# One fetch of the fixed blocks' weights for two phases, and a routing softmax built on tanh

## The chip, the cores and the metric

The kernel runs on one core of a Trainium2 chip. The metric is the device time of one execution in microseconds (us). Below, PE is the TensorE matrix engine (PEld is its weight load), DVE is VectorE, ACT is ScalarE, POOL is GpSimd, and SP is SyncE, whose queue issues most DMA transfers. Line numbers such as L882 are lines of the kernel before.

## The reference

The kernel computes one decoder layer on 32 sequences of 128 tokens with width 128: causal self-attention with 16 heads of 8, cross-attention to a second input, and a mixture of 8 experts of which each token takes 2, each followed by a residual sum and a layer norm. The part that the change touches:

```python
def _moe(x, rw, rb, w1, b1, w2, b2):
    xf = x.reshape(T, D)                                        # 4096 tokens x 128
    router_weights = jax.nn.softmax(xf @ rw + rb, axis=-1)      # over 8 experts
    topw, topi = jax.lax.top_k(router_weights, K)               # K = 2
    topw = jax.nn.softmax(topw, axis=-1)
    combine = zeros((T, E)).at[arange(T)[:, None], topi].add(topw)
    h = gelu(einsum('td,edf->etf', xf, w1) + b1[:, None, :], approximate=False)
    eo = einsum('etf,efd->etd', h, w2) + b2[:, None, :]         # hidden width 512
    return einsum('etd,te->td', eo, combine)

x = layernorm(x + attn(x, x, x, causal=True))
x = layernorm(x + attn(x, encoder_output, encoder_output, causal=False))
x = layernorm(x + moe(x))
```

Each token's two weights are a softmax of the two largest softmax values.

## The kernel before

**Attention.** The 32 sequences form 8 groups of 4. For each group the kernel runs self-attention (`s`) and later cross-attention (`c`). A sequence of one kind is a unit, and the program walks through the units in half-slots (`half_slot`): each gives TensorE half of a new unit's scores (`sc`, L457, whose maxima `m` VectorE takes at L465), half of an older unit's transposed scores (`st`, L450, whose exponentials ScalarE takes at L473 into the tile `pr`), and the values or outputs of a still older one. All other steps of a group (transposes into `kvT`, keys `k`, queries, projection, norm, hand-over `xT0`, routing) are generators. `chain` and `book` put their pieces into half-slots by a table of estimated engine costs, and the emission order is then kept as it is: every engine works through its own instructions in that order.

**Routing.** After cross-attention, `route` (L608 to L653) computes the logits `lg`, their softmax (Exp at L622, normalization at L625 to L627), the largest values `top` and their places `idx`, and the two weights from the difference of the two largest values with Tanh (L640). `place` (L668 to L755) counts tokens per expert and gives each of a token's two rows a slot; `biases` forms `comb`, transposes it on TensorE (`pw`, L597), and writes the residual sum with the weighted expert biases to `x2d`. `scatter` sends rows to their slots in `xs` with indirect DMAs from GpSimd (L762). The routing of the last two groups is emitted beside the expert blocks.

**Blocks.** The groups form two phases of four. The rows of a phase fill 39 blocks of 128 rows. The first 8 blocks of each phase belong to the experts 0 to 7 in order (the fixed blocks, `i < NS`). The expert of each of the other 31 is known only from the routing, and SP reads it from `ph.tab` before it issues the fetch. A block's weights are one row of `wpk` in HBM, packed early in the kernel: 1028 floats on each of 128 partitions, with the first layer, the second layer and 4 bias columns. `fetch_weights` (L822) brings them into a `wd` tile; that tag has `AHEAD + 1`, five, buffers. `Pipeline.run` fetches the weights of block `j + AHEAD`, issues the first layer of block `j` (`ph`, L866, and Gelu, L871), then the second layer of the block before (`po`, L882), which VectorE copies to `ot` (L887) and GpSimd sends to `eo` with an indirect DMA (L889). Rows are fetched (`xt`, L814) and transposed (`px`, L843, copied to `xT` at L858) four blocks at a time. `prepare` fetches the first four blocks' weights six half-slots before the blocks start. `combine` (L950) loads a group's results (`gt`), adds them with the two weights, applies the last norm and stores the output; it starts four blocks after the last block that its group needs.

Of the kernel before, what the change touches and what calls it, by code (L numbers as in the profile page):

```python
# [17 lines left out]
P = 128  # L18
# [35 lines left out]
def bc(ap, axis, n):  # L54

    ap = ap.unsqueeze(axis)
    shape = list(ap.shape)
    shape[axis] = n
    return ap.broadcast_to(shape)
# [3 lines left out]
def kernel(  # L63
# [544 lines left out]
    def route(gr):  # L608
# [11 lines left out]
        nc.vector.tensor_tensor(lg, lg, bc(lm, 2, E), ALU.subtract)  # L620
        yield
        nc.scalar.activation(lg, lg, AF.Exp)  # L622
        yield
        ls = small.tile([P, G], F32, tag="ls", name=f"ls_{gi}")
        nc.vector.tensor_reduce(ls, lg, AX.X, ALU.add)  # L625
        nc.vector.reciprocal(ls, ls)
        nc.vector.tensor_tensor(lg, lg, bc(ls, 2, E), ALU.mult)  # L627
        top = small.tile([P, G, E], F32, tag="top", name=f"top_{gi}")
        idx = small.tile([P, G, E], U32, tag="idx", name=f"idx_{gi}")
        for b in range(G):  # L630
            nc.vector.max(top[:, b, :], lg[:, b, :])
        yield
        for b in range(G):
            nc.vector.max_index(idx[:, b, :], top[:, b, :], lg[:, b, :])


        ex = small.tile([P, G], F32, tag="ex", name=f"ex_{gi}")
        nc.vector.tensor_tensor(ex, top[:, :, 0], top[:, :, 1], ALU.subtract)
        yield
        nc.scalar.activation(ex, ex, AF.Tanh, scale=0.5)  # L640
        idf = small.tile([P, G, 2], F32, tag="idf", name=f"idf_{gi}")
# [9 lines left out]
        yield  # L651
        nc.vector.tensor_scalar(wts[:, 0, bs], ex, 0.5, 0.5, ALU.mult, ALU.add)
        nc.vector.tensor_scalar(wts[:, 1, bs], ex, -0.5, 0.5, ALU.mult, ALU.add)  # L653

# [123 lines left out]
    def pack_biases():  # L778
        pb = mm_tile([P, E * NFC], "pb")
        nc.tensor.transpose(pb, b1, ident[: E * NFC, : E * NFC])  # L780
        b1T = setup.tile([P, E * NFC], F32, name="b1T")
        nc.vector.tensor_copy(b1T, pb)
        nc.sync.dma_start(
            out=wpk[:, :, B1:].rearrange("e p c -> p e c"),
            in_=b1T.rearrange("p (e c) -> p e c", c=NFC),
        )
# [8 lines left out]
    def weights(name):  # L795
        return moe.tile([P, 1, WP], F32, tag="wd", name=f"wd_{name}", bufs=AHEAD + 1)

    class Blocks:
# [23 lines left out]
        def fetch_weights(self, i):  # L822
            if i >= self.n:
                return
            wd = weights(f"{self.ph.p}_{i}")
            if i < NS:
                nc.sync.dma_start(out=wd[:, 0, :], in_=wpk[i])
            else:
                d = i - NS
                e = nc.sync.value_load(self.ph.tab[0:1, d : d + 1], min_val=0, max_val=E - 1)  # L830
                nc.sync.dma_start(
                    out=wd, in_=wpk[bass.ds(e, 1), :, :].rearrange("e p w -> p e w")
                )
            self.w[i] = wd[:, 0, :]

# [24 lines left out]
        def first_layer(self, i):  # L860
            w, name = self.w[i], f"{self.ph.p}_{i}"
            pool, tag = ((ps_sc, "sc"), (ps_st, "st"))[i % 2]
            hid = pool.tile([P, 2, NFC, P], F32, tag=tag, name=f"ph_{name}")[:, 0]
            self.h[i] = moe.tile([P, NFC, P], F32, tag="h", name=f"h_{name}")
            for c in range(NFC):
                nc.tensor.matmul(  # L866
                    hid[:, c, :], lhsT=w[:, c * P : (c + 1) * P],
                    rhs=self.xT[i // XB][:, i % XB, :], start=True, stop=True,
                )
            for c in range(NFC):  # L870
                nc.scalar.activation(  # L871
                    self.h[i][:, c, :], hid[:, c, :], AF.Gelu, bias=w[:, B1 + c : B1 + c + 1]
                )

        def second_layer(self, i):
            if i < 0:
                return
            q, p = i // XB, self.ph.p
            w, h = self.w.pop(i), self.h.pop(i)
            po = mm_tile([P, P], f"po_{p}_{i}")  # L880
            for c in range(NFC):
                nc.tensor.matmul(  # L882
                    po, lhsT=h[:, c, :], rhs=w[:, W2 + c * P : W2 + (c + 1) * P],
                    start=c == 0, stop=c == NFC - 1,
                )
# [14 lines left out]
    class Pipeline:  # L900


        def __init__(self, *blocks):
            self.all = [(k, i) for k in blocks for i in range(k.n)]
            self.quads = [(k, q) for k in blocks for q in range(-(-k.n // XB))]
            self.turned = 0

        def weights(self, j):
            if j < len(self.all):
                k, i = self.all[j]  # L910
                k.fetch_weights(i)

        def prepare(self):
            for j in range(AHEAD):
                self.weights(j)

# [13 lines left out]
        def run(self, beside):  # L930
# [3 lines left out]
            for j, (k, i) in enumerate(self.all):  # L934
                self.weights(j + AHEAD)
                k.first_layer(i)
# [192 lines left out]
    start = max(behind, ready)  # L1129
    at(start - 6, blocks.prepare)  # L1130
    at(start - 1, blocks.first_rows)

    def unit(t):
# [125 lines left out]
```

## Time and profile before

| | |
|---|---|
| runs, median (lowest to highest) | 683.09 us (679.27 to 684.35), 3 runs |
| the profiled execution | 683.11 us |
| its span, first to last instruction | 681.4 us |
| busy share of PE / DVE / ACT / POOL | 87% / 60% / 59% / 54% |
| chain that ended last | PE 59%, DVE 16%, ACT 9%, issue 6%, DMA 6% |
| blocks: first `ph` to the end of the last `po` | 458.93 to 660.83 us |
| phase two: its first `ph` | 578.83 us |
| weights of blocks | 78 transfers of 514 KB, 16 of them for fixed blocks |
| table loads of ScalarE beside blocks | five of 1.28 us, the first at 457.56 |

Lines of the timeline have the start in us, the length in us, the engine, the line and operation, the tiles (written <- read), shapes and a count of merged instructions; in square brackets stands how long the engine was idle before it and what ended that. "issue" means that nothing in the profile shows what it waited for. Lines by stretches of time have, for each engine, the busy us and the number of instructions, then the granted TensorE clock (1.00 is full), the mean busy share of the 16 DMA engines and the GB/s moved. The rows of 40 digits divide the span into slices of 17 us, in tenths of the clock granted and of the DMA engines' time.

### The profile page before, as it was taken

Reading aid. Unit: us, or ns where it says so; the run is one execution under the profiler, and the core shown is the slowest. Engines: PE = TensorE matmul, PEld = TensorE weight load, DVE = VectorE, ACT = ScalarE, POOL = GpSimd, SP = SyncE. Lnnn points to the kernel's source line nnn. Section 1 sums busy time; section 2 is a strip of 40 time slices with the busy share of each in tenths; the row PEclk is TensorE's granted clock in tenths of the full one; section 3 lists DMA queues with packets and bytes.
Section 4 is the critical chain, followed back from the end, with each engine's and each line's share of the span. In section 5 each row is a group of like instructions: output and inputs, shape, how many; then the busy total and the mean of one; then the engine's idle time right before and its main releaser. Section 6 shows DMA issues by size and latency. Waiting matters only on the chain.

```text
span 681.4 us, 21953 instructions
## 1 busy us (share of the span) xinstructions
PE 591.5 (87%) x8863; PEld 486.6 (71%) x8863; DVE 409.2 (60%) x1321; ACT 402.4 (59%) x919; POOL 368.0 (54%) x747
## 2 busy tenths in 40 slices
PE   8898898999998899989999888879888888999970
PEld 6666676777776666776776776768777688989870
DVE  2345555555668866795796786784664435553553
ACT  4166575686676567666767766554653355655651
POOL 3156554444545557447647435454766676555651
PEclk9699999899999999999999999998968899999995
DMA  6010701731010020001001000604667889999972
GB/s 139 20 34 3 137 20 37 201 135 58 2 34 2 11 64 11 2 22 37 26 2 57 10 3 18 218 14 152 209 213 219 299 274 366 371 371 356 356 262 76
DMA packets 48038, 82.48 MB, mean 121 GB/s; under 512 B 7968, under 2 KB 26464, under 8 KB 47936
## 3 DMA queue, kind: packets, MB, share of 16 engines
q1 hardware_dynamic: 42816, 71.57, 33.2%
q0 software_dynamic: 4544, 9.38, 3.8%
q8 instruction: 69, 1.13, 0.7%
q14 instruction: 33, 0.27, 0.1%
q10 hardware_dynamic: 576, 0.13, 0.1%
HBM read 62.15 MB, written 23.10 MB: 125 GB/s over the span
## 4 chain that ended last, share of the span: by engine, by line
PE 59%; DVE 16%; ACT 9%; issue 6%; DMA 6%; POOL 3%; SPq 1%; ACTq 0%; DVEq 0%; another core or an unknown queue 0%; POOLq 0%
PE ph L866 7%; PE po L882 7%; PE st_s L450 6%; PE st_c L450 5%; PE sc_s L437 4%; DVE m_s L465 4%; DMA wd<-wpk 4%; PE po_s L512 3%; DVE m_c L465 3%; PE po_c L512 3%; PE sc_c L457 3%; PE st_s L442 2%; ACT pr_s L473 2%; PE st_c L442 2%; PE sc_s L457 2%
## 5 line engine op out<-in xcount | busy, mean ns | idle before, releaser
L871 ACT ACTIVATE h<-ph,wd 128x128 f32<-128x128 f32 x312 | 88.0, 371 | 79.1 <-issue 45.6
L465 DVE TENSOR_REDUCE m_s<-sc_s 128x8 f32<-128x1024 f32 x64 | 78.3, 1224 | 84.8 <-PE st_s L450 65.0
L477 POOL TENSOR_SCALAR_AFFINE_SELECT pr_s<-pr_s 128x1024 f32<-128x1024 f32 x64 | 69.9, 1092 | 99.4 <-ACT pr_s L473 99.3
L889 POOL DMA_INDIRECT eo<-ot,to x78 | 78.5, 1007 | 66.2 <-DVE acc L974 15.0
L473 ACT ACTIVATE pr_s<-st_s 128x1024 f32<-128x1024 f32 x64 | 65.6, 1026 | 64.1 <-PE st_s L450 59.0
L473 ACT ACTIVATE pr_c<-st_c 128x1024 f32<-128x1024 f32 x64 | 65.7, 1027 | 59.1 <-PE st_c L450 53.7
L465 DVE TENSOR_REDUCE m_c<-sc_c 128x8 f32<-128x1024 f32 x64 | 78.0, 1219 | 32.6 <-PE st_c L450 19.6
L866 PE MATMUL ph<-xT,wd 128*128 128x128 f32 x624 | 89.5, 289 | 9.3 <-DMA wd<-wpk 3.8
L882 PE MATMUL po<-wd,h 128*128 128x128 f32 x624 | 88.1, 287 | 9.8 <-ACT h L871 7.4
L866 PEld LDWEIGHTS ph<-xT,wd 128*128 128x128 f32 x624 | 80.6, 202 | 15.2 <-issue 6.3
L882 PEld LDWEIGHTS po<-wd,h 128*128 128x128 f32 x624 | 80.7, 200 | 11.4 <-ACT h L871 8.6
L457 PE MATMUL sc_c<-k_c,qb_c 32*128 32x128 f32 x1024 | 75.3, 283 | 4.5 <-DVE m_c L465 4.1
L457 PE MATMUL sc_s<-k_s,qb_s 32*128 32x128 f32 x1024 | 78.1, 293 | 0.0
L887 DVE COPY ot<-po 128x128 f32<-128x128 f32 x78 | 22.6, 290 | 83.4 <-PE po L882 59.3
L762 POOL DMA_INDIRECT xs<-x,slots x64 | 64.3, 1005 | 12.7 <-issue 12.1
L450 PE MATMUL st_c<-qb_c,k_c 32*128 32x128 f32 x1024 | 70.2, 272 | 0.2 <-issue 0.2
L450 PEld LDWEIGHTS st_s<-qb_s,k_s 32*128 32x128 f32 x1024 | 69.7, 192 | 0.1
L450 PE MATMUL st_s<-qb_s,k_s 32*128 32x128 f32 x1024 | 69.6, 275 | 0.0
L450 PEld LDWEIGHTS st_c<-qb_c,k_c 32*128 32x128 f32 x1024 | 68.8, 187 | 0.9 <-issue 0.4
L457 PEld LDWEIGHTS sc_s<-k_s,qb_s 32*128 32x128 f32 x1024 | 65.5, 194 | 2.5 <-issue 2.1
L457 PEld LDWEIGHTS sc_c<-k_c,qb_c 32*128 32x128 f32 x1024 | 62.5, 185 | 6.1 <-DVE m_c L465 5.7
L437 PE MATMUL sc_s<-causal,ident 128*128 128x512 bf16 x128 | 39.7, 393 | 13.7 <-DVE m_s L465 10.3
(243 smaller groups left out, 1186.8 us busy)
## 6 DMA issues: line engine op xcount, KB each, us to landing
wd<-wpk SPq DMA_DIRECT2D x78, 514.0 KB
xs<-blank SPq DMA_DIRECT2D x2, 2600.0 KB
xt<-xs SPq DMA_DIRECT2D x20, 260.0 KB
wpk<-in_L_xattn_e_w_dram SPq DMA_DIRECT2D x16, 256.0 KB
gt<-eo SPq DMA_DIRECT2D x8, 512.0 KB
xg<-in_x_dram SPq DMA_DIRECT2D x8, 256.0 KB
eg<-in_ctx_dram SPq DMA_DIRECT2D x8, 256.0 KB
x2d<-base SPq DMA_DIRECT2D x8, 256.0 KB
```

The lines of the kernel that those rows point to most:

```text
L437: nc.tensor.matmul(sc[:, i], lhsT=ident16, rhs=causal, start=True, stop=False)
L450: nc.tensor.matmul(st[:, i, r, :], lhsT=old.group.k[rowsof(g), old.b, :], rhs=old.group.qb[rowsof(g), old.b, r, :], start=False, stop=r == 3,)
L457: nc.tensor.matmul(sc[:, i, r, :], lhsT=new.group.qb[rowsof(g), new.b, r, :], rhs=new.group.k[rowsof(g), new.b, :], start=not new.masked, ...
L465: nc.vector.tensor_reduce(new.m[:, 8 * half : 8 * half + 8], sc.rearrange("p i r k -> p (i r) k"), AX.X, ALU.max,)
L473: nc.scalar.activation(old.pr[:, hs, :], st.rearrange("p i r k -> p (i r) k"), AF.Exp, scale=SCALE)
L477: nc.gpsimd.affine_select(out=old.pr[:, hs, :], in_=old.pr[:, hs, :], pattern=[[0, 8], [1, P]], compare_op=ALU.is_ge, fill=0.0, base=0, ch ...
L512: nc.tensor.matmul(po[VC * r : VC * r + VC, g, :], lhsT=u.group.v[:, u.b, at_v : at_v + VC], rhs=u.pr[:, h, :], start=e == 0, stop=e == 1,)
L762: i = nc.gpsimd.indirect_dma_start(out=xs[ph.p][:, :], out_offset=bass.IndirectOffsetOnAxis(ap=slots[:, k, t : t + 1], axis=0), in_=gr.x2[ ...
L866: nc.tensor.matmul(hid[:, c, :], lhsT=w[:, c * P : (c + 1) * P], rhs=self.xT[i // XB][:, i % XB, :], start=True, stop=True,)
L871: nc.scalar.activation(self.h[i][:, c, :], hid[:, c, :], AF.Gelu, bias=w[:, B1 + c : B1 + c + 1])
L882: nc.tensor.matmul(po, lhsT=h[:, c, :], rhs=w[:, W2 + c * P : W2 + (c + 1) * P], start=c == 0, stop=c == NFC - 1,)
L889: s = nc.gpsimd.indirect_dma_start(out=eo[p][:, :], out_offset=bass.IndirectOffsetOnAxis(ap=self.to[q][:, i % XB : i % XB + 1], axis=0), i ...
```

## The change

There are two edits. The fixed blocks' weights are fetched once, before and while phase one's blocks start, and are kept for phase two. They lie in tiles that attention no longer needs (three `kvT`, three `xT0`, four `k`, two `pr`), as two DMAs per expert, and the bias columns are read from `b1T` in SBUF. The fetches of the other blocks keep the five `wd` buffers; `Pipeline.weights` now fetches, at the start of each block from the third on, until four data-dependent blocks lie between the current block and the next one to be fetched, passing over fixed blocks.

In the routing, the exponential of a logit difference is (1 + t) / (1 - t) with t the Tanh of half the difference. `top` and `idx` are taken from the logit differences instead of from the softmax, and the softmax is formed on the sorted values. Tanh is in the table set that serves the Gelu of the blocks, so ScalarE has no table load for it there.

```diff
@@ route
         nc.vector.tensor_tensor(lg, lg, bc(lm, 2, E), ALU.subtract)
-        yield
-        nc.scalar.activation(lg, lg, AF.Exp)
-        yield
+        top = small.tile([P, G, E], F32, tag="top", name=f"top_{gi}")
+        idx = small.tile([P, G, E], U32, tag="idx", name=f"idx_{gi}")
+        for b in range(G):
+            nc.vector.max(top[:, b, :], lg[:, b, :])
+        yield
+        ex = small.tile([P, G, E], F32, tag="exr", name=f"ex_{gi}", bufs=2)
+        nc.scalar.activation(ex, top, AF.Tanh, scale=0.5)
+        for b in range(G):
+            nc.vector.max_index(idx[:, b, :], top[:, b, :], lg[:, b, :])
+        yield
+        nc.vector.tensor_scalar(lg, ex, -1.0, 1.0, ALU.mult, ALU.add)
+        nc.vector.reciprocal(lg, lg)
+        nc.vector.scalar_tensor_tensor(lg, ex, 1.0, lg, ALU.add, ALU.mult)
         ls = small.tile([P, G], F32, tag="ls", name=f"ls_{gi}")
         nc.vector.tensor_reduce(ls, lg, AX.X, ALU.add)
         nc.vector.reciprocal(ls, ls)
         nc.vector.tensor_tensor(lg, lg, bc(ls, 2, E), ALU.mult)
...
-        yield
-        nc.scalar.activation(ex, ex, AF.Tanh, scale=0.5)
+        d = small.tile([P, G], F32, tag="ex", name=f"d_{gi}")
+        nc.vector.tensor_tensor(d, lg[:, :, 0], lg[:, :, 1], ALU.subtract)
+        yield
+        nc.scalar.activation(d, d, AF.Tanh, scale=0.5)
...
@@ weights of fixed blocks
+    kept = {}
+    def fixed_weights(e):
+        if e not in kept:
+            if e < len(PLACES):
+                w = [act.tile([P, FF], F32, tag=tag, name=f"w{n}_{e}", bufs=bufs[tag])
+                     for n, tag in zip((1, 2), PLACES[e])]
+            else:
+                two = (e - len(PLACES)) % 2
+                if not two:
+                    kept["pr"] = prob.tile([P, 2, 2, FF], F32, tag="pr", name=f"w_{e}")
+                w = [kept["pr"][:, two, n] for n in range(2)]
+            nc.sync.dma_start(out=w[0], in_=wpk[e, :, :W2])
+            nc.sync.dma_start(out=w[1], in_=wpk[e, :, W2:B1])
+            kept[e] = w[0], w[1], kept["b1T"][:, NFC * e : NFC * e + NFC]
+        return kept[e]
+    bufs = {"kvT": 3, "k": 4, "xT0": 3}
+    PLACES = (("kvT", "kvT"), ("kvT", "xT0"), ("xT0", "xT0"), ("k", "k"), ("k", "k"))
@@ Blocks.fetch_weights
+            if i < NS:
+                self.w[i] = fixed_weights(i)
+                return
             wd = weights(f"{self.ph.p}_{i}")
-            if i < NS:
-                nc.sync.dma_start(out=wd[:, 0, :], in_=wpk[i])
...
@@ Pipeline
         def weights(self, j):
-            if j < len(self.all):
-                k, i = self.all[j]
+            while self.fetched < len(self.all):
+                k, i = self.all[self.fetched]
+                behind = sum(n >= NS for _, n in self.all[j : self.fetched])
+                if i >= NS and behind >= AHEAD:
+                    return
                 k.fetch_weights(i)
-        def prepare(self):
-            for j in range(AHEAD):
-                self.weights(j)
+                self.fetched += 1
+        def prepare(self, n0, n1):
+            for k, i in self.all[n0:n1]:
+                k.fetch_weights(i)
+            self.fetched = n1
@@ Pipeline.run
-                self.weights(j + AHEAD)
+                if j > 1:
+                    self.weights(j)
                 k.first_layer(i)
@@ start of the blocks
-    at(start - 6, blocks.prepare)
+    at(start - 6, blocks.prepare, 0, 3)
     at(start - 1, blocks.first_rows)
+    at(start - 1, blocks.prepare, 3, NS - 1)
+    at(start + 1, blocks.prepare, NS - 1, NS)
```

## The prediction

> **What bounds the kernel now.** I read the page's slices first, then the busy time by stretches of 20 us, then each engine's instructions in order of time where the two edits act. The profiled execution took 683.11 us (span 681.4, 1.7 around it); the median of the runs is 683.09, so sums are made against 683.1.
>
> ```profile
> PEclk9699999899999999999999999998968899999995
> DMA  6010701731010020001001000604667889999972
> 540.00:560.00 20.00, 18.26 (x120) 16.15 (x121) 6.83 (x29) 9.29 (x33) 14.15 (x27) 0.83 0.76 242
> ...
> 580.00:600.00 20.00, 18.90 (x165) 18.41 (x164) 10.58 (x44) 12.82 (x44) 11.34 (x20) 1.00 1.02 374
> ```
>
> Until about 440 us attention keeps TensorE at nine tenths and the DMA engines nearly idle. The expert blocks run from 459 to 661 in two regimes: to 560 routing runs beside them and the granted clock dips to 0.83; from 560 the DMA engines are full (share 1.02, 374 GB/s). The second regime on TensorE:
>
> ```profile
> 626.90 1.06 PE L882 MATMUL po<-wd,h 128*128 128x128 f32 x8
> 629.03 1.13 PE L866 MATMUL ph<-xT,wd 128*128 128x128 f32 x8 [1.07 <-DMA wd<-wpk]
> ...
> 634.89 1.06 PE L866 MATMUL ph<-xT,wd 128*128 128x128 f32 x8
> 635.79 1.06 PE L882 MATMUL po<-wd,h 128*128 128x128 f32 x8
> 636.68 1.06 PE L866 MATMUL ph<-xT,wd 128*128 128x128 f32 x8
> ...
> 646.10 1.13 PE L866 MATMUL ph<-xT,wd 128*128 128x128 f32 x8 [1.67 <-DMA wd<-wpk]
> ```
>
> An undisturbed block takes 1.79 us (634.89 to 636.68), 1.90 with its quarter of the 0.44 for four transposes. Now and then a first layer waits for its weights. The first regime, ScalarE and then TensorE:
>
> ```profile
> 477.40 1.28 ACT L622 ACT_TABLE_LOAD   x1
> 478.69 0.23 ACT L622 ACTIVATE lg<-lg 128x32 f32<-128x32 f32 x1
> 478.94 1.28 ACT L871 ACT_TABLE_LOAD   x1
> 480.24 2.17 ACT L871 ACTIVATE h<-ph,wd 128x128 f32<-128x128 f32 x8
> ...
> 478.19 1.06 PE L866 MATMUL ph<-xT,wd 128*128 128x128 f32 x8
> 480.66 1.26 PE L882 MATMUL po<-wd,h 128*128 128x128 f32 x8 [1.42 <-ACT h L871]
> ...
> 485.44 0.28 PE L597 MATMUL pw<-ident,comb 128*32 128x128 f32 x1 [1.30 <-DVE comb L594]
> ```
>
> Two table loads hold back one block's Gelu, and TensorE waits 1.42; but 4 us later it waits again, for VectorE's comb.
>
> **Weights of phase two's fixed blocks.** Removed: 8 transfers of 514 KB, 4.1 MB or 11.0 us of full DMA engines at 374 GB/s. On the path lies less. From the first ph of phase two (578.83) to the end of the last po (660.83) pass 82.0 us; undisturbed work is 39 x 1.79 + 8 x 0.44 + 0.5 for the last three transposes + about 0.5 for the last Gelu = 74.3. Of the 7.7 lost, the waits laid to weights (0.34, 0.76, 1.07, 1.67, each with 0.17 of modelled overlap) are 4.5; one late Gelu at 613 costs 1.1; the rest is scattered. That is the gain's ceiling: 4.5, or 6 with some scatter.
>
> What remains? The `wd` tag still has five buffers, and the new rule stops at four data-dependent weights ahead. During the eight fixed blocks only those four are in flight, so the saved bytes become idle DMA time, and the fifth transfer (block 12 of the phase) goes out at about 594.5. Block 8 would start at 578.83 + 8 x 1.79 + 2 x 0.44 = 594.0 instead of 594.76. A block moves 514 + 65 (rows in) + 64 (rows out) + 105 (its share of four combines) = 748 KB, 2.0 us at 374 GB/s against TensorE's 1.90. 27 weights at 2.0 need 54 us; from 594.5 to block 38's start at 594.0 + 30 x 1.90 = 651 there are 56.5. So a full lead at block 8 lasts nearly to the end; I leave 0.5 of waits and take **-4.0** (ends -1.0, if bursts of combine loads break the lead, and -6.0).
>
> In phase one the same eight weights are fetched as 16 transfers of 256 KB, still HBM to SBUF. The first six wait for attention tiles already read by 440. The `k` and `pr` fetches wait on SP's queue for the last scores and values (about 456; the last one 463), with the second row fetch and the first data-dependent weights behind them. Rows went out at 438.40 and are needed at 469.26; 2 MB before them take 5.6 us, so they land near 463. Cover 6 us: 0 (ends 0 and +2). The fetch one step later in program order costs 0: SP waited for the same second layer either way. The bias read from b1T costs 0: one ScalarE operand for another.
>
> **Table loads.** Gone are four of 1.28 us, in two pairs beside blocks. The Trainium skill (ScalarE: Activation LUTs, What ACT_TABLE_LOAD costs) puts a switch at a 1.28 load plus a 1.38 drain, 2.66. The row agrees on the load, but from 477.40 to the next h at 480.24 lie 2.84 us with two loads and the Exp: no room for drains. By the rule four switches are 10.6 us of ScalarE, by the row 5.1. On TensorE the first pair is worth 1.58 (478.19 + 0.89 to 480.66), the second 0.45 (508.78 to 509.23). Before the first can count, VectorE must keep up.
>
> **VectorE.** Added: three operations per group (scale, reciprocal, multiply on 128x32), 0.21 us apart like the ls and lg rows, 0.63; eight groups 5.0 us. Moved: max and max_index ahead, tanh's operands and one-hots one half-slot earlier. In the first six groups, beside attention, VectorE is 60 to 75% busy and carries 16% of the chain: 6 x 0.63 x 0.16 = **+0.6** (ends 0 and 3.8). Before the first block VectorE runs without a break from 449 to 458.87, where xT ends: +0.63 and two wts rows +0.23 go ahead of xT, and 0.47 of waiting for rs_c is filled: **+0.4** (-0.5 to +0.9).
>
> The costly place is group six's route, 473 to 485.4:
>
> ```profile
> 480.77 1.62 DVE L748 TENSOR_TENSOR sums<-sums,part 128x31 f32<-128x31 f32 x1
> ...
> 485.19 0.19 DVE L594 TENSOR_TENSOR comb<-comb 128x32 f32<-128x32 f32 x1
> 485.30 0.08 DVE L634 MATCH_VALUE_LOAD idx<-top,lg 128x8 f32 x1
> ```
>
> VectorE has no gap here. Eight max_index rows (0.65) move ahead of comb, three operations (0.63) and d (0.1) come in: +1.4. L748 takes 1.62 instead of 0.19 beside GpSimd's L583 (481.15 to 482.34), and an engine arriving later waits less: I take +0.7. TensorE, 1.58 earlier, reaches pw at 482.5 and waits to 486.1. **The first table gain is hidden by VectorE: 0, and +0.7 remains** (-1.3 to +1.4). At the second pair comb comes 0.45 later and the gap of 0.45 goes: 0.
>
> **The clock.** That joins two short waits into one of 3.6 us. The Trainium skill (TensorE: Matmul & The Clock Gate, What's actually happening) lets the clock fall after an idle window of about 3.4 us. This trace is stricter:
>
> ```profile
> 540.17 2.08 PE L882 MATMUL po<-wd,h 128*128 128x128 f32 x8 [2.06 <-issue]
> 542.18 2.07 PE L602 MATMUL pb<-b2g,wT 32*128 32x512 f32 x2
> ```
>
> After 2.06 us matmuls take twice as long, for 7 us; after 2.33 (519.72) for 3.6; after 1.42 and 1.30 not. By the rule 3.6 is just at the edge, half a case; by the row it is certain, 1.8 to 3.5 us. TensorE idles for 3.6 us again between 493 and 497, where delay can vanish: **+0.9** (ends 0 and +3.5).
>
> Sum: -4.0 + 0.6 + 0.4 + 0.7 + 0.9 = -1.4: **681.7 us**.
>
> **Rivals.** *The stalls all go* (faster): weights -6.0, both table gaps count (-1.6, -0.4) because VectorE, its POOL collision displaced, keeps up, attention +0.4: 675.5. For it: the waits are real and the ScalarE delay direct. Against: VectorE's unbroken row. Chance 0.22.
>
> *VectorE's longer routing cools TensorE* (slower): the wait at pw falls wholly in one window, the half clock lasts 7 us as at 540, and group seven's route, 1.4 later, does the same: 2 x 3.5, + 1.4 + 0.6 + 0.4, weights only -1.5: 691.0. It decides once that wait passes 2.06 us. For it: the order on VectorE; against: later waits of 'issue' in the same stretch absorb delay. Chance 0.14.
>
> *The saved transfers do nothing*: with five buffers the dynamic blocks fall back to 2.0 us and weights give -1.0: 684.7; part of no change.
>
> **How the numbers follow.** Runs spread over 679.3 to 684.4, so about 1% is what a measurement can tell. Likeliest 681.7 at 0.64, its own range 677 to 686; with the others the range is 674 to 690. Faster by over 1% 0.22, within 0.64, slower 0.14.
>
> **What would show it.** q1's bytes fall by 4.1 MB; the DMA share drops below 0.6 for some 10 us in phase two's first blocks; waits for wd there vanish and return at most late. One table load near 457 remains. pw of group six waits over 3 us for comb, with half-clock matmuls after. I am wrong if waits for wd continue from block 12 on, if pw does not wait, or if ScalarE's unexplained 'issue' pauses (4.06 at 519.30, 5.40 at 539.75) shift with the new instruction count.

## The result and the profile after

The changed kernel took 687.64 us (median of 12 runs, 682.96 to 690.49) against 682.98 for the kernel before (12 runs, 677.65 to 694.38): a ratio of 1.0077, 95% interval [1.0054, 1.0100]. It is slower by 0.8%. The forecast was 681.7, slightly faster; the time lies inside the range of 674 to 690, but the sign is wrong. Medians here and below are over all runs; a ratio leaves out the runs more than 1.5% above the fastest of their kernel, so it is not the quotient of two medians.

The profiled execution has a span of 685.4. By stages, from the instructions of TensorE (first `ph` of the blocks, first `ph` of phase two, end of the last `po`):

| stage | before | after |
|---|---|---|
| start to the first ph | 458.9 | 460.1 |
| phase one | 119.9 | 123.6 |
| phase two | 82.0 | 81.0 |
| what follows | 20.6 | 20.7 |

The page's slices of granted clock and DMA share, after the change:

```profile
PEclk9999999999999999999999998989899699999995
DMA  6111805350010020010001001437176789689972
```

And the busy times of two stretches (stretch and length, busy us of TensorE, weight load, VectorE, ScalarE and GpSimd, then granted clock, DMA share and GB/s):

```profile
580.00:600.00 20.00, 18.82 (x167) 18.45 (x166) 11.41 (x46) 13.03 (x45) 11.40 (x22) 1.00 0.69 249
596.00:600.00 4.00, 4.00 (x36) 3.84 (x36) 2.34 (x9) 3.15 (x11) 2.10 (x4) 1.00 0.16 49
```

The weights part shows as forecast: the main queue moves 67.34 MB instead of 71.57, the DMA share of 580 to 600 falls from 1.02 to 0.69, and just before the fifth data-dependent fetch of phase two it is down to 0.16. Phase two is shorter, by less than forecast. The loss is in phase one. TensorE there and later, in order of time:

```profile
482.15 1.06 PE L910 MATMUL po<-w,h 128*128 128x128 f32 x8
488.06 0.39 PE L597 MATMUL pw<-ident,comb 128*32 128x128 f32 x1 [4.86 <-DVE comb L594]
488.25 1.92 PE L894 MATMUL ph<-xT,wd 128*128 128x128 f32 x8
489.96 1.91 PE L910 MATMUL po<-w,h 128*128 128x128 f32 x8
...
508.84 1.48 PE L910 MATMUL po<-wd,h 128*128 128x128 f32 x8 [2.80 <-ACT h L899]
...
530.98 2.07 PE L910 MATMUL po<-wd,h 128*128 128x128 f32 x8 [4.58 <-ACT h L899]
...
625.07 1.13 PE L894 MATMUL ph<-xT,wd 128*128 128x128 f32 x8 [1.30 <-DMA wd<-wpk]
...
648.71 1.16 PE L894 MATMUL ph<-xT,wd 128*128 128x128 f32 x8 [1.10 <-DMA wd<-wpk]
```

Before, the wait at `pw` was 1.30 us and the rows behind it took 1.06; now it is 4.86 and they take 1.92. (The `comb` is that of group five, made while group six is routed; the prediction's "pw of group six" is this row.) The waits of phase two for weights are three instead of four, 3.2 us instead of 3.8. Three rows of VectorE on the way to `comb`, in order of time:

```profile
481.71 2.00 DVE L749 TENSOR_TENSOR which<-end,d_at 128x248 f32<-128x248 f32 x1
...
484.51 0.35 DVE L634 RECIPROCAL lg<-lg 128x32 f32<-128x32 f32 x1
...
487.82 0.19 DVE L594 TENSOR_TENSOR comb<-comb 128x32 f32<-128x32 f32 x1
```

Three rows of ScalarE, the same way:

```profile
459.18 1.28 ACT L899 ACT_TABLE_LOAD   x1
...
508.30 0.23 ACT L629 ACTIVATE ex<-top 128x32 f32<-128x32 f32 x1 [3.74 <-DVE top L624]
...
530.56 2.18 ACT L899 ACTIVATE h<-ph,wd 128x128 f32<-128x128 f32 x8 [6.96 <-issue]
```

One table load is left beside the blocks. In its place ScalarE stands 3.74 us before its first tanh, because that now reads VectorE's `top`, with a Gelu behind it in order; that Gelu is what TensorE waited 2.80 us for at 508.84. And VectorE needs longer to `comb`: from `moved`, the operation that opens this stretch (before 473.05, after 473.94), to the end of `comb` (485.38 and 488.01) it took 12.33 us and takes 14.07.

This pair of profiles shows what the late `comb` costs at its place, not that it makes the 0.8%. Counted from block 0, block 10 starts 3.7 us later than before (35.5 against 31.8), as much as the whole of phase one loses. But at block 12 the changed kernel is 3.1 us ahead (40.6 against 43.7): the kernel before idles there and then runs at half clock, so the delay vanishes in the stretch where the prediction had let it. At block 20 it is still 3.0 ahead, and from there it falls back by 6.7. Much of that is late Gelus, such as the one at 530.56 that nothing in the trace holds back. The prediction had named a shift of these pauses as a sign of being wrong. Which part makes the loss had to be found by experiments.

### The profile page after: what moved, and what is told of

The parts are those of the page before. It is cut to its first block, busy times and chain, and to the rows that moved or that the text cites. A ratio compares the mean times of both kernels' runs of the same rounds, so it can differ in the third digit from the quotient of the medians.

```text
span 685.4 us, 21912 instructions
## 1 busy us (share of the span) xinstructions
PE 583.7 (85%) x8812; PEld 488.5 (71%) x8863; DVE 416.2 (61%) x1345; ACT 399.2 (58%) x915; POOL 368.2 (54%) x747
## 3 DMA queue, kind: packets, MB, share of 16 engines
q1 hardware_dynamic: 42816, 67.34, 31.7%
## 4 chain that ended last, share of the span: by engine, by line
PE 54%; DVE 19%; ACT 10%; issue 8%; POOL 4%; DMA 4%; SPq 0%; ACTq 0%; another core or an unknown queue 0%; DVEq 0%; POOLq 0%
PE po L910 7%; PE ph L894 7%; PE st_s L450 6%; PE st_c L450 5%; DVE m_s L465 4%; DVE m_c L465 3%; PE po_c L512 3%; PE po_s L512 3%; PE sc_s L437 3%; PE st_s L442 3%; PE sc_c L457 3%; ACT pr_s L473 3%; ACT pr_c L473 2%; PE st_c L442 2%; DMA wd<-wpk 2%
## 5 line engine op out<-in xcount | busy, mean ns | idle before, releaser
L899 ACT ACTIVATE h<-ph,wd 128x128 f32<-128x128 f32 x248 | 70.5, 372 | 68.3 <-issue 42.9
L457 PE MATMUL sc_c<-k_c,qb_c 32*128 32x128 f32 x1024 | 78.6, 292 | 5.6 <-DVE m_c L465 5.0
L910 PE MATMUL po<-wd,h 128*128 128x128 f32 x496 | 71.0, 290 | 13.3 <-ACT h L899 13.0
L910 PEld LDWEIGHTS po<-wd,h 128*128 128x128 f32 x496 | 65.1, 203 | 14.6 <-ACT h L899 14.0
L894 PE MATMUL ph<-xT,wd 128*128 128x128 f32 x496 | 71.7, 291 | 4.4 <-DMA wd<-wpk 3.2
L457 PE MATMUL sc_s<-k_s,qb_s 32*128 32x128 f32 x1024 | 74.2, 283 | 0.3
L450 PE MATMUL st_c<-qb_c,k_c 32*128 32x128 f32 x1024 | 73.9, 280 | 0.2 <-issue 0.2
L894 PEld LDWEIGHTS ph<-xT,wd 128*128 128x128 f32 x496 | 65.0, 204 | 9.2 <-issue 3.4
L457 PEld LDWEIGHTS sc_s<-k_s,qb_s 32*128 32x128 f32 x1024 | 62.0, 185 | 1.7 <-issue 1.3
L442 PEld LDWEIGHTS <-ones 32*128 32x128 bf16 x256 | 13.9, 91 | 49.1 <-issue 45.8
```

Source lines behind the costliest of these rows:

```text
L442: nc.tensor.matmul(st[:, i], lhsT=ones16[rowsof(g), :], rhs=old.mq[rowsof(g)], start=True, stop=False,)
L450: nc.tensor.matmul(st[:, i, r, :], lhsT=old.group.k[rowsof(g), old.b, :], rhs=old.group.qb[rowsof(g), old.b, r, :], start=False, stop=r == 3,)
L457: nc.tensor.matmul(sc[:, i, r, :], lhsT=new.group.qb[rowsof(g), new.b, r, :], rhs=new.group.k[rowsof(g), new.b, :], start=not new.masked, ...
L894: nc.tensor.matmul(hid[:, c, :], lhsT=w[:, c * P : (c + 1) * P], rhs=self.xT[i // XB][:, i % XB, :], start=True, stop=True,)
L899: nc.scalar.activation(self.h[i][:, c, :], hid[:, c, :], AF.Gelu, bias=b[:, c : c + 1])
L910: nc.tensor.matmul(po, lhsT=h[:, c, :], rhs=w[:, c * P : (c + 1) * P], start=c == 0, stop=c == NFC - 1,)
```

## The experiments

Four of them first split the change. The theory was the prediction's: the weights gain about 4 us, the routing's longer VectorE chain gives some back. The rival was that TensorE's cooling behind the late `comb` is the main price. `E1` is the weights part alone, `E2` the routing part alone, `E3` the routing part with the old order:

```
-        nc.scalar.activation(lg, lg, AF.Exp)
-        yield
+        ex0 = small.tile([P, G, E], F32, tag="exr", name=f"ex0_{gi}", bufs=2)
+        nc.scalar.activation(ex0, lg, AF.Tanh, scale=0.5)
+        yield
+        nc.vector.tensor_scalar(lg, ex0, -1.0, 1.0, ALU.mult, ALU.add)
+        nc.vector.reciprocal(lg, lg)
+        nc.vector.scalar_tensor_tensor(lg, ex0, 1.0, lg, ALU.add, ALU.mult)
```

(max, max_index and the one-hots stay where they were.) `E4` is the weights part with one more data-dependent weight ahead, which the five buffers allow:

```
-                if i >= NS and behind >= AHEAD:
+                if i >= NS and behind > AHEAD:
```

> Only the weights edit; the routing is that of the kernel before, with its Exp and its table loads. Theory A (the routing edit is what costs): this part alone is worth -1 to -2 us, ratio to before 0.997 to 1.000, and phase two's blocks (first ph to the last po) take about 81 us as in the changed kernel, against 82.0 before. Theory B (the weights edit costs: its fetches between 456 and 470 us, and one block less of lead for the others): ratio 1.005 or more, and the late Gelus of the changed kernel in phase one are here too.

> Only the routing edit; weights as in the kernel before. Theory A: ratio 1.008 to 1.014 (all of the slowdown, and the weights' small gain is missing); group six's pw waits over 3 us for comb, with half-clock matmuls after it, and one Gelu of group seven's stage waits behind the Tanh of ex. Theory B: ratio 0.995 to 1.002.

> Weights as before; in the routing only the Exp is replaced by Tanh and three VectorE operations, and max, max_index and the Tanh of the two weights stay where they were. It tells the moved order from the added operations. If the order costs (max and max_index ahead of comb, and ScalarE's Tanh waiting for top in front of a Gelu): ratio 0.996 to 1.003, pw of group six waits under 3 us. If the three added operations cost: ratio close to that of the routing edit alone, 1.006 or more.

> Only the weights edit, with one more data-dependent fetch allowed ahead, so that the fifth wd buffer is filled while phase two's fixed blocks run. If the five buffers and the late sixth fetch are what turns the saved bytes into idle DMA time: phase two's blocks 1 to 2.5 us shorter than with the weights edit alone, ratio to before 0.994 to 0.998. If the DMA engines are the limit in the second half anyway, no difference from the weights edit alone.

Measured, against a median of 683.88 for the kernel before in the same job:

| kernel | median us | ratio | 95% interval |
|---|---|---|---|
| E1 weights only | 683.40 | 0.9951 | [0.9914, 0.9987] |
| E2 routing only | 690.33 | 1.0023 | [0.9984, 1.0061] |
| E3 tanh in place | 686.68 | 0.9996 | [0.9963, 1.0028] |
| E4 five ahead | 681.64 | 0.9957 | [0.9925, 0.9990] |

The weights part gains 0.49%, 3.4 us: close to the 4.0 of the prediction, and more than the 1 to 2 expected of this run. A fifth weight ahead adds nothing to it that can be measured. The routing part gains nothing, and what it costs this job left open: by the medians 0.9%, by the ratio 0.2%, with an interval that leaves out the 0.8 to 1.4% expected if the routing made all of the loss. 0.9951 times 1.0023 is not the 1.0077 of the whole. The profile of E2 has the late `comb` all the same, with waits of 4.81 and 3.40 us at the two `pw`. E3 lies where it was expected if the order costs, but its first wait was 3.96 us, not under 3.

The second job put the whole change beside two variants and a candidate. In `E6` both edits are made, with the tanh in the old place as in E3. In `E7` and `E8` the scale and shift of x2 in the last two groups go from GpSimd to VectorE:

```
-        nc.gpsimd.tensor_tensor(x2, gr.y, bc(lng[1], 1, G), ALU.mult)
+        eng = nc.vector if gr.gi >= 6 else nc.gpsimd
+        eng.tensor_tensor(x2, gr.y, bc(lng[1], 1, G), ALU.mult)
         yield
-        nc.gpsimd.tensor_tensor(x2, x2, bc(lnb[1], 1, G), ALU.add)
+        eng.tensor_tensor(x2, x2, bc(lnb[1], 1, G), ALU.add)
```

E7 is that on top of the whole change, E8 on top of E4 (old routing).

> The changed kernel itself, again, beside the same runs of before as the next three. The weights alone measured 0.9951 and the routing alone 1.0023, which multiply to 0.9974, while the whole change measured 1.0077. Theory A (the two parts hinder each other: with the weights at hand early, VectorE's longer routing and ScalarE's tanh become the bound of phase one): 1.006 to 1.010 again. Theory B (no interaction, and the routing's cost was understated in its own run): 1.000 to 1.004, and the routing alone would read higher when repeated.

> The weights part with the exponential replaced by tanh in its old place: the same number of new operations, but max, max_index and the one-hots stay where they were before the change, and ScalarE's tanh does not wait for VectorE's max. Theory order (the new order of VectorE and ScalarE makes the cost): at least 3 us below the changed kernel of the same batch, ratio 0.995 to 0.999, waits of the second layer for h back under 2 us each. Theory operations (the three added operations per group make the cost, wherever they stand): within 1.5 us of the changed kernel.

> The changed kernel, with the scale and shift of x2 in the last two groups on VectorE instead of GpSimd, so that no GpSimd operation stands beside VectorE's route of those groups. Theory collision (rows of VectorE blocked 1.8 us each beside GpSimd hold comb back): slots and which shrink from 1.97 and 2.00 to about 0.2 and 0.4, two rows of about 0.6 each come in, comb 2 us earlier, the first wait of pw 4.9 down to about 3, and the time 1 to 3 us below the changed kernel. Theory none: the blocked rows only move, comb stays within 0.5 us, the time stays.

> A candidate against both kernels: the weights part with five data-dependent weights ahead, the routing of before (Exp and its table loads), and the scale and shift of x2 of the last two groups on VectorE. Five ahead with the routing of before measured 0.9957. Theory collision: comb of group six 1.5 us earlier, its wait under 1 us, ratio 0.993 or lower. Theory none: 0.995 to 0.997, as without the move.

| kernel | median us | ratio | 95% interval | waits at the two pw | phase one |
|---|---|---|---|---|---|
| before | 656.58 | | | | |
| E5 whole change | 672.68 | 1.0202 | [1.0132, 1.0272] | 4.08, 3.39 | 114.0 |
| E6 both, in place | 663.89 | 1.0117 | [1.0070, 1.0164] | 3.23, 2.85 | 109.2 |
| E7 whole, x2 on VectorE | 655.94 | 1.0021 | [0.9976, 1.0066] | 2.38, 2.26 | 102.3 |
| E8 weights, five ahead, x2 on VectorE | 652.16 | 0.9934 | [0.9884, 0.9984] | none, none | 99.6 |

In this job the kernel before took 27 us less than in the first two, and the change cost more. By the ratios E6 lies 0.85% (5.6 us) below the whole change, on the side of order, but the two intervals overlap and it is not below 1.000 as expected. E7 lies 1.8% (12 us) below, where 1 to 3 us were expected. E8's 0.9934 lies between its two expectations (0.993 or lower; 0.995 to 0.997), and its interval covers both. Each step that brings `comb` earlier shortens phase one, and by far more than the wait itself. E5 and E7 differ by 2.8 us in the two waits and by 11.7 in phase one. Where the rest goes is seen on TensorE. Its rows in E7 around the two waits, in order of time:

```profile
480.87 0.29 PE L598 MATMUL pw<-ident,comb 128*32 128x128 f32 x1 [2.38 <-DVE comb L595]
480.99 1.70 PE L895 MATMUL ph<-xT,wd 128*128 128x128 f32 x8
482.49 1.91 PE L911 MATMUL po<-w,h 128*128 128x128 f32 x8
484.33 1.25 PE L603 MATMUL pb<-b2g,wT 32*128 32x512 f32 x2
...
503.03 0.28 PE L598 MATMUL pw<-ident,comb 128*32 128x128 f32 x1 [2.26 <-DVE comb L595]
503.15 1.06 PE L895 MATMUL ph<-xT,wd 128*128 128x128 f32 x8
```

The wait of 2.38 us is followed by matmuls at half speed (granted clock 0.50 from 481.22 to 484.63), the one of 2.26 by none. The whole change, with waits of 4.08 and 3.39, has nine microseconds of half-speed work behind each (shown below). The collision itself, first in three rows of VectorE in E5:

```profile
470.09 1.97 DVE L738 TENSOR_TENSOR slots<-si,ri 128x8 uint32<-128x8 uint32 x1
...
475.91 2.00 DVE L749 TENSOR_TENSOR which<-end,d_at 128x248 f32<-128x248 f32 x1
...
482.00 0.19 DVE L594 TENSOR_TENSOR comb<-comb 128x32 f32<-128x32 f32 x1
```

GpSimd's two operations on x2 in the same stretch of E5:

```profile
470.75 1.28 POOL L581 TENSOR_TENSOR x<-y_c,lng 128x512 f32<-128x512 f32 x1
...
476.44 1.19 POOL L583 TENSOR_TENSOR x<-x,lnb 128x512 f32<-128x512 f32 x1
```

VectorE again, in E7, where these two are its own:

```profile
470.42 0.17 DVE L739 TENSOR_TENSOR slots<-si,ri 128x8 uint32<-128x8 uint32 x1
470.82 0.69 DVE L582 TENSOR_TENSOR x<-y_c,lng 128x512 f32<-128x512 f32 x1 [0.23 <-issue]
...
475.96 0.41 DVE L750 TENSOR_TENSOR which<-end,d_at 128x248 f32<-128x248 f32 x1
...
480.62 0.19 DVE L595 TENSOR_TENSOR comb<-comb 128x32 f32<-128x32 f32 x1
```

In E5 `slots` and `which` last until the GpSimd operation ends or just past it (472.06 against 472.03, 477.91 against 477.63), and take 1.97 and 2.00 us; without it 0.17 and 0.41. By the profile they start 0.66 and 0.53 us before it; spans on GpSimd are rough. The two operations that move in cost 0.69 and 0.68. From `moved` to `comb` that is 14.05 us in E5 (468.14 to 482.19) and 12.35 in E7 (468.46 to 480.81).

The third job asked whether the clock or the wait is the price, by giving TensorE something to do. `E11` is the whole change plus, ahead of the transpose into `pw`:

```
         pw = mm_tile([G * E, P], f"pw_{gi}")
+        for _ in range(26 if gi in (5, 6) else 0):
+            nc.tensor.matmul(pw, lhsT=ident[:, : G * E], rhs=ident, start=True, stop=True)
         nc.tensor.transpose(pw, w[:, 0].rearrange("p b e -> p (b e)"), ident)
```

> The kernel before, profiled beside the next three, since the times of before differ between chips (683 and 657 us). Theory clock: comb waits of at most 1.5 us and no stretch of half-speed matmuls after pw, so phase one 100 to 106 us if this chip shows few late Gelus, 118 to 122 if it shows as many as the first profile.

> The changed kernel beside the next two. Ratio 1.006 to 1.010 where before takes about 683 us, 1.013 to 1.027 where it takes about 657.

> The changed kernel with 26 matmuls (32x128 out, fp32, 0.11 us each: 2.9 us) whose results are overwritten, put ahead of the transposes pw of groups five and six, so that TensorE works while it waits for comb. Theory clock (the price of the late comb is the half-speed stretch after the wait: 9.2 us of half speed behind a wait of 4.08 us and 9.2 behind one of 3.39 in the last profile of the changed kernel, 4.6 us lost each): waits at pw under 1.5 us, no half-speed rows after them, 4 to 9 us below the changed kernel of the same batch. Theory wait (the price is the wait itself, 4.1 + 3.4 us, which the filling cannot shorten): within 1.5 us of the changed kernel.

> The routing part alone once more, now beside the whole change. Theory clock: it carries the waits at pw of 4.8 and 3.4 us and the half-speed stretches by itself, so its ratio lies above that of the whole change by about the 0.5% that the weights gain: 1.012 to 1.03 where before takes about 657 us, 1.002 to 1.015 where it takes about 683. Theory interaction (the weights' transfers are needed for the loss): 0.998 to 1.004.

Against 656.0 for the kernel before: the whole change (E10) 664.49, ratio 1.0123 [1.0080, 1.0166]; kept warm (E11) 662.37, 1.0110 [1.0060, 1.0160]; routing only (E12) 664.20, 1.0130 [1.0083, 1.0177]. The routing part alone carries the whole loss, so no interaction with the weights is needed; that it should lie 0.5% above the whole change is not resolved by these intervals. E11 was badly sized, as TensorE's row ahead of the first `pw` shows:

```profile
475.82 5.87 PE L598 MATMUL pw<-ident 128*32 128x128 f32 x52
```

One call is two rows of the trace, so the filling lasted 5.87 us where 4.1 and 3.4 were to be filled. Phase one went from 112.5 to 107.1 us all the same, but the times differ by less than their intervals. TensorE in the kernel before (E9, one run of 663.21, at the upper end of its scatter, phase one 105.1) shows what the waits were:

```profile
477.89 0.28 PE L597 MATMUL pw<-ident,comb 128*32 128x128 f32 x1 [1.07 <-DVE comb L594]
478.02 1.06 PE L866 MATMUL ph<-xT,wd 128*128 128x128 f32 x8
...
519.58 0.40 PE L597 MATMUL pw<-ident,comb 128*32 128x128 f32 x1 [2.56 <-DVE comb L594]
519.77 1.92 PE L866 MATMUL ph<-xT,wd 128*128 128x128 f32 x8
```

The kernel before thus lies close below the edge: 1.07 and 1.65 us at the first two, and at the third, in this run, 2.56 with half speed behind it. (The profile of the weights alone in the next job, E15, has 1.07, 1.63 and 1.58 there, and no half speed.)

`E13` and `E17` fill 14 and 11 calls, `range({5: 14, 6: 11}.get(gi, 0))`. `E15` repeats the weights alone, `E16` is E6 with x2 on VectorE.

> The changed kernel with overwritten matmuls ahead of the pw of groups five and six again, but sized to the wait: 14 and 11 calls, of two rows each at 0.113 us, so 3.2 and 2.5 us against waits of 4.1 and 3.4 (the 26 calls of the run before filled 5.87 us, 1.8 and 2.5 more than the waits). Theory clock: waits of about 0.9 us left, no half-speed rows after pw, comb where it was; 9 us less of half-speed loss, so 6 to 9 us below the changed kernel of the same batch. Theory wait (half speed after a wait costs nothing that is not given back later): within 2 us of the changed kernel.

> The changed kernel beside the three others. Ratio 1.010 to 1.022 where before takes about 656 us, 1.005 to 1.010 where it takes 683.

> The weights part alone, beside the whole change. Theory sum (the parts add): 0.990 to 0.996, phase two 2 to 4 us shorter than with the old weights (82 to 83.6), waits at pw under 1.7 us. Theory early blocks (the fetches of the fixed weights beside the last attention units cost what phase two saves on a chip with few late Gelus): 0.998 to 1.003.

> Both edits, with tanh in the old place of the exponential and the scale and shift of x2 of the last two groups on VectorE: comb should come 1.7 us earlier than in the same kernel with x2 on GpSimd (waits at pw 3.23 and 2.85 there), so waits of 1.5 and 1.2 us, no half-speed rows, ratio 0.988 to 0.996. If the collision is not the cause of the lag, waits stay above 2.5 us and the ratio at 1.008 to 1.014.

| kernel | median us | ratio | 95% interval | runs |
|---|---|---|---|---|
| before | 659.28 | | | 43 |
| E13 whole, waits filled | 665.49 | 1.0155 | [1.0096, 1.0213] | 6 |
| E14 whole change | 663.16 | 1.0117 | [1.0057, 1.0177] | 6 |
| E15 weights only | 656.14 | 0.9954 | [0.9921, 0.9987] | 22 |
| E16 both, in place, x2 on VectorE | 657.37 | 0.9979 | [0.9943, 1.0016] | 22 |

E13 was a miss: its profile had phase one at 105.9 us against 112.5 in E14, but its six runs showed no gain. So the pair was run once more, with more runs.

> The changed kernel with the filled waits once more (14 and 11 calls). Its one profile had phase one 6.7 us shorter than the changed kernel's beside it, but six runs of each had means of 664.4 and 664.5 us, with single runs from 658.5 to 668.8. Theory clock: this time 3 to 8 us below the changed kernel, and phase one again near 106 us. Theory given back: phase one of the profile again 5 us or more shorter up to block 20, but the lead lost to late transfers and late Gelus from block 21 on, and the mean within 2 us of the changed kernel.

> The changed kernel beside it: ratio 1.005 to 1.020, waits at pw of 4.1 and 3.4 us with nine microseconds of half speed behind each.

Against 657.2 for the kernel before: E18, the whole change, 666.50 (17 runs), ratio 1.0115 [1.0076, 1.0155]; E17, waits filled, 660.16 (22 runs), ratio 1.0042 [1.0012, 1.0071]. The filled kernel is faster by 0.73% of the time before; the means of all runs are 666.1 and 661.0, 5.1 us apart. E11 and E13, with six runs each, did not show it. TensorE in E18, from the first of the two waits on:

```profile
476.63 0.40 PE L597 MATMUL pw<-ident,comb 128*32 128x128 f32 x1 [4.08 <-DVE comb L594]
476.82 1.91 PE L894 MATMUL ph<-xT,wd 128*128 128x128 f32 x8
478.52 1.91 PE L910 MATMUL po<-w,h 128*128 128x128 f32 x8
480.37 2.07 PE L602 MATMUL pb<-b2g,wT 32*128 32x512 f32 x2
482.37 2.08 PE L894 MATMUL ph<-xT,wd 128*128 128x128 f32 x8
484.24 1.73 PE L910 MATMUL po<-wd,h 128*128 128x128 f32 x8
485.80 0.24 PE L694 MATMUL count<-chosen,ones 128*128 128x8 bf16 x4
```

The same work on TensorE in E17:

```profile
474.09 3.24 PE L598 MATMUL pw<-ident 128*32 128x128 f32 x28
478.24 0.28 PE L599 MATMUL pw<-ident,comb 128*32 128x128 f32 x1 [0.91 <-DVE comb L594]
478.36 1.06 PE L896 MATMUL ph<-xT,wd 128*128 128x128 f32 x8
...
483.18 0.24 PE L696 MATMUL count<-chosen,ones 128*128 128x8 bf16 x4
```

From the `ph` behind `pw` to `count` lie 8.98 us in E18 and 4.82 in E17: 4.2 us of half speed lost. At the second `pw` it is 9.13 (503.77 to 512.90) against 4.82: 4.3. The filling did not make `comb` come earlier, it only kept the clock. The granted clock of E18 around the first of the two waits (stretch and length, busy us of TensorE with its instructions, then clock, DMA share and GB/s):

```profile
471.98:475.39 3.41, 0.56 (x6) 1.00 0.08 24
475.39:478.81 3.42, 2.18 (x11) 0.50 0.11 35
478.81:482.22 3.41, 3.41 (x10) 0.50 0.18 61
482.22:485.63 3.41, 3.41 (x16) 0.50 0.34 116
485.63:489.05 3.42, 3.42 (x38) 1.00 0.57 183
```

The clock changes in steps. In all 20 profiles every stretch of half clock begins on a grid of 3.41 us, which lies differently against the start of each, and those that end before the program does last one to four steps of it. While the blocks run, all 34 steps at full clock with less than 1.4 us of work on TensorE were followed by half clock, and none of the 949 with more than 1.8; of the 24 between, 10 were. So the length of one wait does not decide. In E7 the wait of 2.38 us left a step with 1.03 us of work, while that of 2.26 fell into two steps with 2.48 and 2.08. In the kernel before, pauses of 0.64, 1.36 and 1.62 us left 1.28 us in one step, and half clock followed for 10.24 us (495.72 to 505.96). The filling of E17 raised the step ahead of `pw` from the 0.56 us of E18 to 2.54.

Not all of the 8.5 us reaches the end. The start of block n's first layer, counted from block 0's:

| block | 8 | 10 | 16 | 18 | 30 | 31 | 39 (phase two) |
|---|---|---|---|---|---|---|---|
| E18 whole change | 27.3 | 36.6 | 54.2 | 63.5 | 91.9 | 95.3 | 113.5 |
| E17 waits filled | 26.8 | 31.9 | 48.8 | 53.7 | 81.0 | 86.9 | 105.2 |

The lead is 9.8 us at block 18, 11.0 at block 30, and 8.4 at block 31. There E17 stands still once (2.98 us, for a Gelu), and three engines in order of time say why. GpSimd:

```profile
532.94 0.97 POOL L768 DMA_INDIRECT xs<-x,slots  x1 [0.22 <-issue]
...
534.27 1.04 POOL L335 TENSOR_TENSOR rs_m<-rs_m,mhalf 128x4 f32<-128x4 f32 x1
```

VectorE, which waited for that:

```profile
535.35 0.16 DVE L337 SCALAR_TENSOR_TENSOR rs_m<-mv_m,rs_m 128x4 f32<-128x4 f32 x1 [6.12 <-POOL rs_m L335]
```

ScalarE, which waited for VectorE:

```profile
535.55 0.88 ACT L340 ACTIVATE acc<-acc,rs_m 128x128 f32<-128x128 f32 x2 [4.84 <-DVE rs_m L337]
```

A Gelu stands behind `acc` on ScalarE, `acc` behind VectorE's `rs_m`, that behind GpSimd's, which stands behind indirect DMAs issued 1.28 us apart (530.39, 531.67, 532.94). So part of the gain in phase one is given back there. That a TensorE which comes earlier must meet this queue is argued, not tested.

Two more answers come from the fourth job. The weights alone again give 0.9954. And E16, where the tanh stays, `comb` is back in time (waits of 1.58 and 1.46, no half speed, phase one 100.3 in its profile) and no table load is left between blocks, lies at 0.9979, no better than the weights without any tanh (0.988 to 0.996 was expected). It still has the three operations per group that VectorE needs in place of the exponential. Taking the table loads away at that price is worth nothing that these runs can measure, even with `comb` in time.

The version that beats both kernels is E8: 652.16 us against 656.58 for the kernel before and 672.68 for the changed one, all in one job, ratio to before 0.9934 [0.9884, 0.9984]. It keeps the weights part and the old exponentials. Whether the move of x2 adds to E1's and E4's 0.995 can't be told from these intervals.

## Why the prediction was wrong, point by point

**Weights, -4.0: right in size, in part in mechanism.** Alone they gave -3.4 us (0.49% of 683.9) and -3.0 (0.46% of 659.3). Phase two takes 79.5 us on average in the profiles of the 15 runs with the weights part and 82.4 in the five without. The bytes and the empty DMA stretch came as forecast (share 0.44 from 590 to 600 us of the profile after). The lead did not last nearly to the end. In the first 25 us of phase two the waits for `wd` are 1.7 us on average without the part and none with it, but the later ones are 1.5 and 2.7, where 0.5 was to be left. So the waits account for little of the 2.9 us; where the rest comes from is not located. One detail was also off: the fifth data-dependent fetch of phase two went out at 601.67, where 594.5 plus the shift of the phase's start (4.9) makes 599.4; on SP's queue it stands behind an output store at 600.49. E4 shows that allowing one fetch more ahead is not worth a measurable time.

**Fetches in phase one and the first groups' VectorE, 0 and +0.6: not seen.** The scatter of the attention stage (first `ph` between 446.8 and 460.4 over all kernels) hides both.

**First table gain hidden by VectorE: right.** Block 7 starts 2.1 us earlier after block 0 than before (21.2 against 23.3), and block 8 1.6 us later (28.2 against 26.6).

**"+0.7 remains": mis-sized.** `comb` came 1.74 us later by VectorE's own chain. The estimate of +1.4 was nearly right; the discount, that the collision with GpSimd would be met later and cost less, was not. It moved from `sums` (1.62) to `which` (2.00) at its full size; and the reciprocal on 128x32 took 0.35 where I had taken the 0.18 of the 128x4 row.

**"The clock: +0.9" and "at the second pair: 0": the step that failed.** The wait was forecast at over 3 us with half-clock rows behind, and so it was; what failed is the price. With the +0.7 for the wait I put 1.6 us on the late `comb`. I let half of the half clock vanish in the idling between 493 and 497, and I gave the second `pw` nothing, although group seven's route is the same longer chain. In the profile after, half clock behind the first `pw` costs 2.1 us (from the `ph` behind `pw` to `count` 6.91 us instead of 4.82), which lies inside my 1.8 to 3.5, and block 10 is 3.7 us late before the delay vanishes. But the idling is not the program's own: in E9, the kernel before in a later job, block 12 starts 35.7 us after block 0 instead of 43.7, and nothing there absorbs a delay. In the later jobs each of the two waits costs 4.2 us of half speed beside itself, and the routing part alone cost 1.30% (E12), 8.5 us, where its terms (0.6, 0.4, 0.7 and 0.9) sum to 2.6. How much of the 0.8% of the first comparison came this way stays open: in the job of E1 to E4, where the kernel before took as long, the routing part alone gave 0.2%, and behind block 20 the two profiles differ mostly by late Gelus.

The rival "VectorE's longer routing cools TensorE" had the mechanism, the two places and, with +7.9 us, the size of three later comparisons: E10, E14 and E18 measured +1.15 to +1.23% of some 657, 7.6 to 8.1. (The first had +0.8%, about 5 us, and E5 +2.0%; its -1.5 for the weights was too small.) It deserved more than 0.14. Its row, 7 us of half speed behind 2.06 of idling, was in the prediction; its "against", later waits that absorb, was taken from a profile in which other late work cooled TensorE already.

The Trainium skill's rule on the clock (TensorE: Matmul & The Clock Gate, What's actually happening) lets the clock fall after an idle window of about 3.4 us, and calls the window free-running. The grid of 3.41 us in the traces agrees with the second part, not with the first: a step with 1.50 us of work was enough (E1, 480.72 to 484.13). Weighing the rule as half a case was too kind, and ordering the trace's gaps by their length missed the three short pauses before 495.72.

**Not in the prediction:** the tanh `ex` waits for VectorE's `top` in ScalarE's order, ahead of a Gelu (3.74 us, and 2.80 on TensorE in the profile after). Its share was not separated from the later `comb`: E6, which undoes both by the old order, is 0.85% below E5, with waits still at 3.23 and 2.85.

## What to carry to other kernels

Where a change makes one engine's in-order chain longer, find the instruction of TensorE that waits for its end, and price the wait at its own length plus the half-speed stretch behind it; here waits of 3.4 to 4.1 us cost 4.2 us more each, and waits of 1 to 1.7 us nothing more. What counts is how much work TensorE has in each step of the clock's grid. By the figures of these traces (an estimate: a step of 3.41 us, and 1.4 to 1.8 us of work in it), a lone wait below some 1.6 us cannot bring the clock down, one above some 4.0 must, and between them its place on the grid decides; several short pauses in one step add up. Such a price can be taken off without shortening the chain, by matmuls with an overwritten result sized to the wait: in the one pair with enough runs that returned 0.73 of the 1.15% lost. And read whether a saved stall (a table load) has another wait right behind it: removing it, at the price of some work on VectorE, was worth nothing measurable even where that wait was short.

## What the hardware showed that was not expected

The same kernel's time depends on the job: the kernel before had medians of 683.0 and 683.9 us in two jobs and 656.0 to 659.3 in the four others. The jobs of 683.9 and of 657.2 carry the same chip number, so that it differs between chips, as one expectation says, is not shown. In the six profiles of the slower two jobs (before, after, E1 to E4) ScalarE's Gelus in phase one start late with no releaser in the trace, three to eight times by 2 us or more ("issue": 3.98 us at 504.81 of before), with waits of TensorE and its half speed behind them; in the other fourteen it is at most three times. The cause is not found. It may be why the change cost 0.8% there and 1.2 to 2.0% elsewhere, since TensorE is cooled in that stretch either way; this is argued, not tested.

Small VectorE operations beside a GpSimd operation on 128x512 lasted until that ended: 128x8 integers 1.97 us instead of 0.17, 128x248 floats 2.00 instead of 0.41. And the length of the half clock does not follow that of the wait. It was three steps (10.24 us) behind waits of 3.4 to 4.1 us in four profiles of the whole change and one of the routing alone, two (6.83) behind the 4.86 of the profile after, and one behind the 2.38. In E18 a first step full of work left the clock at half, in the profile after one brought it back; why is open.
